# A new order of the work behind the last attention of a four-layer network, with products that nobody reads

## The chip, the cores and the metric

The kernel runs on one core of one Trainium2 chip, as one launch. The metric is the device time of an execution in microseconds (us). The engines are called by short names: PE is TensorE (PEld its weight loads), DVE is VectorE, ACT is ScalarE, POOL is GpSimd, and SP is SyncE, which here only orders transfers. Each engine works through its own queue in order. An instruction at the head of a queue that waits for a semaphore holds up all behind it.

## The reference

The input `x` has the shape [4, 56, 56, 128] in float32: 4 images of 3136 tokens with 128 channels. Four layers follow one another; all products are in single precision in the reference.

```python
x = neighbourhood_attention_and_mlp(x)                    # layer 0
x = x + gated_recurrence(group_norm(x))                   # layer 1, 16 steps
t = tokens(x)
t = t + softmax_attention(norm(t))                        # layer 2
t = t + top2_of_8_experts(norm(t))                        # layer 2, "mixture"
t = t + distance_attention(norm(t))                       # layer 3
t = t + experts_choose_tokens(norm(t))                    # layer 3
```

The last two matter here.

- Distance attention: Q, K and V are products of the tokens. The scores are exp(-|q - k|^2), and a softmax over them weighs V. Where all distances are large, every score is near zero, the softmax is uniform, and the result is the mean of V over the image.
- Expert choice: a router gives each token 64 logits; softmax runs over the tokens of an image. Each of 64 experts picks the 8 tokens of an image with the largest share, and the weighted sum of these ("pooled") goes through its own two layers, 129 to 512 with gelu, then 513 to 128. The result times each token's share is added to that token's row of the output.

## The kernel before

A tile is 112 tokens (`P`); an image has 28 tiles in 7 groups (`NG`) of 4 (`GT`). All images stay in SBUF as `env.x[b]`. The work on images 0 to 2 of layers 2 and 3 runs in the background of the attention of later images. What the change moves is the work on the last image, behind the last attention, where nothing is left to run beside it. It stands in a `tc.manual_schedule` block: the order in the program is the order in the queues of PE, DVE, ACT and POOL.

The order of that block before the change:

1. The last group of `Mixture`. `all_experts(g, j)` multiplies tile j by all 8 expert matrices (`y_ps`, L1563, two PSUM tiles of four experts), gates them (ACT at L1570 for j = 1 and 3, DVE at L1576 for j = 0 and 2) and adds them up (L1582, L1585). Then the normalization for layer 3 (`xn`, L1677 on POOL and L1682 on ACT), transposes (`xT_ps`, L207) and the queries and keys.
2. `FarAttention.mean()` (L1869 to L1876): the mean of V. `add(g)` (L1881) adds it to x, groups 0 to 2 on DVE, groups 3 to 6 on POOL.
3. `ExpertChoice.steps`, with a step function for each of these names: `statistics(g)` (sums for the norm), `root(groups)` (inverse standard deviation; groups 0 to 2 are "early", 3 to 6 "late"; DVE, in twelve instructions, then the offset at L2296), `store` (rows of x to DRAM, for the gather), `tokens(g)` (xn), `turned(g)` (transposes, copied to `zT` at L2311), `logits(g)` (L2316), `choose` (the 8 best of each expert, and four indirect DMAs on POOL at L2344 that fetch their rows), `marked` (which tokens are chosen), `weighed`, `gather` (copies the fetched rows and weighs them, L2372 to L2378), `pooled` (L2383 to L2388).
4. `experts()`: 16 steps of 4 experts for all four images. `first(q)` is the first layer (`h_ps`, L2431, copied at L2438), `turned(q)` the transposes, bias and gelu (L2444 to L2459), `second(q)` the second layer (`o_ps`, L2465, copied to `found` at L2471) and four small transfers of `found` into `out`, one for each image (L2478). The weights come in 32 lots of 1 MB, two for each step, into 9 buffers; `more` orders the next on SP (L2252) when a buffer is free. `second` runs two steps behind `first`.
5. `far.decide()` (L1921 to L1934) looks whether all distances were large; if not, another branch repeats the attention in full.
6. `scatter()`: for each pair of images, a product that picks the last results (L2501), the bias (L2504), then for each group products of the shares with the results (`y_ps`, L2518). Half of the results of most groups is copied by ACT (L2527) and added to x by POOL (L2528); the others are added by DVE (L2530). Each [112, 4, 128] block goes out from SP (L2531).

Beside these there are bound tiles: a matrix of |q - k|^2 must be bounded to decide step 5. `bounds(g, c, parts)` multiplies 32 rows of q by k (`d_ps`, L1850), and then either DVE takes the maximum (`tensor_reduce`, L1856) or ACT a sum of relus (L1862). For the last image there are 175 such tiles in 91 lists called `halves`. `beside(by, n)` puts the next n lists at a place of the order, where `by` is "scalar" (all on ACT) or "both" (alternating DVE and ACT). The lists that are left are spread over the steps of `experts()`, every third as "scalar".

The normalization of layers 2 and 3 for one group of tokens is in `span_norms`: DVE works out variance and mean, POOL takes the power -0.5 (L1662), and DVE forms the offset from it:

```python
nc.gpsimd.tensor_tensor(rs, var, env.exponent[:P, :n], ALU.pow)
out["off"] = off = small.tile([P, n], F32, tag=f"g_off{n}_{places}", name="g_off")
nc.vector.scalar_tensor_tensor(off, mean2, -0.5, rs, ALU.mult, ALU.mult)
```

It is called for a single group at 17 places, 15 of them beside attention.

Of the kernel before, what the change touches and what calls it, by code (L numbers as in the profile page):

```python
# [924 lines left out]

def moments(env, pool, tag, st):
# [510 lines left out]
class Mixture:  # L1437
# [41 lines left out]
    def parts(self, b, span, places):  # L1479
# [73 lines left out]
        def all_experts(g, j):  # L1553
            gate = held["gate"][:, span.index(g) * GT + j, :]
            gated = sp.tile([P, NE, C], F32, tag="gated", name="gated")
            by_scalar = shared and j % 2
            for i in range(2):
                if by_scalar:
                    pool, tag = (flow.ps_scores, "s") if j == 1 else (flow.ps_sums, "o")
                    y_ps = pool.tile([P, 4, C], F32, tag=tag, name="y_ps")  # L1560
                else:
                    y_ps = flow.one([P, 4, C], "y_ps")
# [4 lines left out]
                if by_scalar:  # L1567
# [79 lines left out]
def span_norms(env, small, b, span, places, shift=0.0):  # L1647
# [4 lines left out]
    def take():  # L1652
# [5 lines left out]
        if n > GT:  # L1658
            inverse_root(env, small, var, rs)
        else:  # L1660
            nc.vector.tensor_scalar(var, var, 1e-5, None, ALU.add)  # L1661
            nc.gpsimd.tensor_tensor(rs, var, env.exponent[:P, :n], ALU.pow)  # L1662
        out["off"] = off = small.tile([P, n], F32, tag=f"g_off{n}_{places}", name="g_off")
        nc.vector.scalar_tensor_tensor(off, mean2, -0.5, rs, ALU.mult, ALU.mult)  # L1664
# [542 lines left out]
class ExpertChoice:  # L2207
# [46 lines left out]
    def pieces(self, b, places="d"):  # L2254
# [5 lines left out]
        for g in range(NG):  # L2260
# [5 lines left out]
            costing(5.0, steps["choose"]), costing(5.0, steps["marked"]),  # L2266
            *[costing(0.7, lambda g=g: steps["weighed"](g)) for g in range(NG)],
# [3 lines left out]
    def steps(self, b, places, norms_of):  # L2271
# [20 lines left out]
        def root(groups):  # L2292
            of = slice(groups[0] * GT, (groups[-1] + 1) * GT)
            mean2, var = moments(env, sp, f"c{len(groups)}", st[:, of, :])
            inverse_root(env, sp, var, rs[:, of])
            nc.vector.scalar_tensor_tensor(off[:, of], mean2, -0.5, rs[:, of], ALU.mult, ALU.mult)  # L2296
# [53 lines left out]
        def marked():  # L2350
# [8 lines left out]
            nc.vector.reciprocal(inverse, total)  # L2359
# [20 lines left out]
        def pooled():  # L2380
# [13 lines left out]
            logits=logits, choose=choose, marked=marked, weighed=weighed, gather=gather,  # L2394
            pooled=pooled,
        )

    def experts(self, ctx, pool, units, others=()):
# [19 lines left out]
        h, g, used = {}, {}, set()  # L2418
# [42 lines left out]
        def second(q):  # L2461
# [14 lines left out]
            for b in range(B):  # L2476
                at = b % 2 * EC + ET * q
                nc.sync.dma_start(self.outs[b // 2][at : at + ET], by_image[b])  # L2478

        others = Paced(list(others))  # L2480
        slots = 3 * (NQ + 2)
        for q in range(NQ + 2):
            others.step((3 * q + 1) / slots)
# [3 lines left out]
            others.step((3 * q + 2) / slots)  # L2487
            if 0 < q <= NQ:
                turned(q - 1)
            others.step((3 * q + 3) / slots)  # L2490
            if q > 1:
                second(q - 2)
                more(2 * (q - 2) + 1)

    def scatter(self):

        env, nc, flow = self.env, self.env.nc, self.flow
        for pair in range(2):
# [4 lines left out]
            bias = self.late.tile([2 * EC, C], F32, tag="c_bias", name="c_bias")  # L2503
            nc.vector.tensor_scalar(bias, self.bias2, self.inverse[pair], None, ALU.mult)  # L2504
            nc.vector.scalar_tensor_tensor(
                out, out, self.inverse[pair], bias, ALU.mult, ALU.add
            )
            for g in range(NG):
                tiles = slice(g * GT, (g + 1) * GT)
# [12 lines left out]
                for half in range(2):  # L2522
                    b = 2 * pair + half
                    x = env.x[b][:, tiles, :]
                    if half and g not in (3, NG - 1):
# [355 lines left out]
def run_all(pieces):  # L2881
    for piece in pieces:
        piece()


def layers_of_safe_scores(env: Env, f, soft):
    with ExitStack() as ctx:
# [84 lines left out]
        choice, far = held["choice"], held["far"]  # L2972
# [8 lines left out]
        ]  # L2981

# [5 lines left out]
        with tc.manual_schedule(  # L2988
# [6 lines left out]
            beside("scalar", 5)  # L2995
            run_all(tail[:6])
            run_all(tail[6:10])
# [4 lines left out]
            choice.weights(more, range(UNITS))  # L3002
            mean()
# [3 lines left out]
            def each(name, groups):  # L3007
                run_all([lambda g=g: of[name](g) for g in groups])
# [3 lines left out]
            for g in early:  # L3012
                add[g]()
                of["statistics"](g)
                beside("scalar", 1)
            of["root"](early)
            of["store"](early)
            each("statistics", late)
            beside("scalar", 1)
            of["tokens"](0), of["tokens"](1), of["turned"](0), of["logits"](0)  # L3020
            of["root"](late)
            of["store"](late)
            of["turned"](1), of["tokens"](2), of["logits"](1), of["turned"](2), of["logits"](2)
# [96 lines left out]
```

## Time and profile before

| what | us |
|---|---|
| median of 3 runs | 2468.28 (2467.14 to 2473.53) |
| the profiled execution, its own time | 2469.86 |
| its span in the trace | 2467.9 |
| PE busy | 2337.2 (95%) |
| DVE busy | 1806.8 (73%) |
| ACT busy | 1560.5 (63%) |
| POOL busy | 289.6 (12%) |
| work behind the last attention, 2247.05 to the end | 220.85 |

The span is what the trace covers; the execution's own time is 2 us longer. The profile is one execution. The page's second part shows the busy share in 40 equal slices of the span, as digits in tenths; PEclk is the clock that TensorE was granted. Other views give busy time of each engine in chosen stretches, groups of instructions, waits, the chain of work that ended last, and a timeline.

### The profile page before, as it was taken

The numbers are of one execution on the slowest core, as the hardware profiler recorded it, in microseconds if no ns is written. First come the engines' busy times: TensorE is split into PE (matmuls) and PEld (weight loads), VectorE is DVE, ScalarE is ACT, GpSimd is POOL, SyncE is SP. The second block draws the span as 40 slices with busy tenths as digits, with TensorE's granted clock in tenths as the row PEclk, the third lists the DMA queues.
The fourth block names the chain that finished last, engine by engine and source line by source line (L and its number), as shares of the span: only waits on it lengthen the run. The fifth ranks groups of instructions, "written<-read, shape, count | busy, mean of one in ns | idle before, by whom it ended". The sixth has DMA issues, their size and how long they took to land.

```text
span 2467.9 us, 38789 instructions
## 1 busy us (share of the span) xinstructions
PE 2337.2 (95%) x14357; PEld 1256.4 (51%) x14357; DVE 1806.8 (73%) x4798; ACT 1560.5 (63%) x3382; POOL 289.6 (12%) x578
## 2 busy tenths in 40 slices
PE   5999999999999999999999999999999998997585
PEld 3777777775555555555554444445444433343134
DVE  5566899983898859699678777854788676775554
ACT  3899889875675646666432556575545566764583
POOL 4323354320000000000000000100000001012202
PEclk9999999999999999999999999999999998998587
DMA  6000000000000000000000010000000010101585
GB/s 143 14 10 2 2 2 2 2 2 9 1 1 1 1 1 0 1 1 1 12 1 0 1 27 1 5 1 1 1 1 1 1 27 5 27 5 53 151 304 177
DMA packets 65642, 61.42 MB, mean 25 GB/s; under 512 B 17048, under 2 KB 60915, under 8 KB 61348
## 3 DMA queue, kind: packets, MB, share of 16 engines
q1 hardware_dynamic: 64932, 57.80, 8.2%
q8 instruction: 115, 1.88, 0.3%
q0 software_dynamic: 512, 1.06, 0.2%
q14 instruction: 83, 0.68, 0.1%
HBM read 45.83 MB, written 12.90 MB: 24 GB/s over the span
## 4 chain that ended last, share of the span: by engine, by line
PE 63%; DVE 6%; ACT 3%; DMA 2%; POOL 1%; issue 1%; SPq 0%; DVEq 0%; ACTq 0%; POOLq 0%
PE s_ps L2055 20%; PE o_ps L2138 20%; PE y_ps L1563 7%; PE d_ps L1850 3%; PE xT_ps L207 2%; PE g_ps L1196 2%; DMA lot<-in_L_ffn_lots 1%; PE l_ps L2316 1%; ACT d_ps L1862 1%; PE y_ps L2079 1%; PE q_ps L1814 1%; PE z_ps L2031 1%; PE l_ps L1523 1%; ACT xn L1682 1%; DVE found L1856 1%
## 5 line engine op out<-in xcount | busy, mean ns | idle before, releaser
L2062 ACT ACTIVATE e<-s_ps 128x448 f32<-128x448 f32 x688 | 366.9, 542 | 501.4 <-PE s_ps L2055 495.9
L2055 PE MATMUL s_ps<-zT,xnT 128*128 128x448 f32 (+1 forms) x1400 | 648.7, 553 | 0.0
L2138 PE MATMUL o_ps<-e,keep 128*128 128x448 f32 (+1 forms) x1376 | 647.3, 553 | 0.0
L2138 PEld LDWEIGHTS o_ps<-e,keep 128*128 128x128 f32 (+1 forms) x1376 | 241.8, 190 | 218.4 <-issue 217.9
L2055 PEld LDWEIGHTS s_ps<-zT,xnT 128*128 128x128 f32 (+1 forms) x1400 | 241.4, 189 | 214.0 <-issue 194.3
L1862 ACT ACTIVATE d_ps<-d_ps,half 128x448 f32<-128x448 f32 (+1 forms) x394 | 238.5, 607 | 80.9 <-PE d_ps L1850 79.8
L1856 DVE TENSOR_REDUCE found<-d_ps 128x1 f32<-128x448 f32 x306 | 185.7, 618 | 86.8 <-PE d_ps L1850 84.8
L1563 PE MATMUL y_ps<-experts,xnT 128*112 128x512 f32 x448 | 216.3, 607 | 0.0
L1576 DVE TENSOR_TENSOR gated<-y_ps,gate 112x512 f32<-112x512 f32 x220 | 148.4, 685 | 34.1 <-PE y_ps L1563 31.8
L1850 PE MATMUL d_ps<-q_near,k_near 32*128 32x448 bf16 (+1 forms) x700 | 138.1, 379 | 20.9 <-ACT d_ps L1862 13.7
L1582 DVE TENSOR_TENSOR gated<-gated 112x512 f32<-112x512 f32 x330 | 150.7, 464 | 3.3
L207 PE MATMUL xT_ps<-ident,xn 112*128 112x112 f32 x672 | 117.3, 282 | 35.2 <-ACT xn L1682 27.1
L207 PEld LDWEIGHTS xT_ps<-ident,xn 112*128 112x128 f32 x672 | 80.3, 147 | 114.2 <-ACT xn L1682 60.0
L1662 POOL TENSOR_TENSOR g_rs<-var,exponent 112x4 f32<-112x4 f32 x17 | 17.9, 1054 | 993.3 <-DVE var L1661 882.3
L1563 PEld LDWEIGHTS y_ps<-experts,xnT 128*112 128x112 f32 x448 | 77.2, 180 | 98.6 <-issue 62.2
L1850 PEld LDWEIGHTS <-k_near 32*128 32x128 bf16 (+1 forms) x700 | 32.2, 92 | 182.1 <-issue 168.9
L675 DVE TENSOR_TENSOR e<-e,band 112x1792 f32<-112x1792 f32 (+3 forms) x56 | 100.0, 1789 | 15.3 <-ACT e L668 15.3
L1682 ACT ACTIVATE xn<-x,g_off,g_rs 112x128 f32<-112x128 f32 x220 | 93.2, 486 | 28.0 <-DVE g_off L1664 13.1
L780 PE MATMUL f_ps<-w_fc,h 128*112 128x128 f32 x896 | 104.8, 274 | 1.9 <-ACT h L771 1.6
L780 PEld LDWEIGHTS f_ps<-w_fc,h 128*112 128x112 f32 x896 | 99.8, 177 | 5.2 <-ACT h L771 4.8
L766 PE MATMUL h_ps<-zT,w_fc 128*128 128x448 f32 x224 | 88.9, 540 | 0.6 <-ACT zT L760 0.6
L668 ACT ACTIVATE e<-s_ps 112x1792 f32<-112x1792 f32 (+3 forms) x56 | 82.7, 1477 | 5.6 <-PE s_ps L659 2.5
(427 smaller groups left out, 3936.9 us busy)
## 6 DMA issues: line engine op xcount, KB each, us to landing
lot<-in_L_ffn_lots SPq DMA_DIRECT2D x32, 1024.0 KB
out_x<-x SPq DMA_DIRECT2D x28, 224.0 KB
x<-in_x SPq DMA_DIRECT2D x3, 1568.0 KB
rows<-x SPq DMA_DIRECT2D x3, 1568.0 KB
x<-in_x SPq DMA_DIRECT2D x7, 224.0 KB
parts<-in_waves SPq DMA_DIRECT2D x8, 173.0 KB
out<-found SPq DMA_DIRECT2D x60, 2.0 KB
rows<-x SPq DMA_DIRECT2D x1, 896.0 KB
```

The source lines that it names most:

```text
L207: self.nc.tensor.transpose(ps[:, j * P : (j + 1) * P], xn[:, j, :], self.ident[:P, :P])
L780: nc.tensor.matmul(f_ps[:, j, :], h[:, k, j * P : (j + 1) * P], w_fc2[:, k, :], start=(k == 0), stop=(k == 3),)
L1563: nc.tensor.matmul(y_ps, held["xnT"][g][:, j * P : (j + 1) * P], self.experts[:, 4 * i : 4 * i + 4, :], start=True, stop=True,)
L1576: nc.vector.tensor_tensor(gated[:, some, :], y_ps, gate[:, some].unsqueeze(2).to_broadcast([P, 4, C]), ALU.mult,)
L1582: by.tensor_tensor(gated[:, :n, :], gated[:, :n, :], gated[:, n : 2 * n, :], ALU.add)
L1682: env.nc.scalar.activation(xn[:, j, :], env.x[b][:, g * GT + j, :], AF.Identity, bias=norm["off"][:, i : i + 1], scale=norm["rs"][:, i : i ...
L1850: nc.tensor.matmul(d, held["k"][part, 128 * c : 128 * c + n], held["q"][g][part, :], start=True, stop=True,)
L1856: nc.vector.tensor_reduce(self.found[:, self.most : self.most + 1], d, AX.X, ALU.max)
L1862: nc.scalar.activation(d, d, AF.Relu, bias=self.half[:n], accum_out=self.found[:n, self.sums : self.sums + 1],)
L2055: nc.tensor.matmul(s_ps[i * n : (i + 1) * n, :GW], self.xnT[:, at : at + n], zT, start=True, stop=True,)
L2062: nc.scalar.activation(e[:n], s_ps[:n, :GW], AF.Exp)
L2138: nc.tensor.matmul(sums[:, :GW], self.keep[:n, k, :], e[:n], start=(k == 0 and g - 1 not in pairs), stop=last,)
```

## The change

- A new function `power_on_gpsimd` makes the inverse root and the offset on POOL. It is used for every single group in `span_norms`, and for both roots of the last image.
- In the last mixture group, tiles j = 2 and 3 are gated by ACT for the first four experts and by DVE for the other four; j = 1 stays on ACT.
- The order behind the attention is written anew. Ahead of the mixture stand 2 lists of bound tiles and not 5. The statistics of the late groups come together, and then the late root; the seven groups of the router follow in an order with the xn of one or two groups ahead. `products` and `with_norms` of the last group (queries, keys and their norms) stand around `choose` and `marked`; the reciprocal of the softmax's sum is a step of its own, `inverted`. The six "both" lists ahead of `gather` give way to three "scalar" ones. `experts()` gets 79 lists, all "both": 72 tiles on DVE and 79 on ACT, where it was 48 and 91.
- 165 products `warm`, bf16, 128x128 by 256 columns, write PSUM tiles that nobody reads. They stand at thirteen places between the start of the block and `gather`.
- In `experts()`, `second` runs one step behind `first` (17 slots and not 18). The small `out` transfers move from SP's queue to POOL's. The biases for the scatter are made on POOL at the step q = 1.
- `far.decide` moves from ahead of `scatter` into its first pair, ahead of group 3. The path by ACT and POOL is taken for three groups of each pair and not five.

The diff, cut to its core:

```diff
+def power_on_gpsimd(env, mean2, var, rs, off, shift=0.0):
+    nc = env.nc
+    p, n = var.shape
+    nc.vector.tensor_scalar(var, var, 1e-5, None, ALU.add)
+    nc.vector.tensor_scalar(mean2, mean2, -0.5, None, ALU.mult)
+    nc.gpsimd.tensor_tensor(rs, var, env.exponent[:p, :n], ALU.pow)
+    nc.gpsimd.tensor_tensor(off, mean2, rs, ALU.mult)
+    if shift:
+        nc.gpsimd.tensor_scalar(off, off, 1.0, shift, ALU.mult, ALU.add)
...
-            by_scalar = shared and j % 2
+            by_scalar = shared and j == 1
...
-                if by_scalar:
+                if by_scalar or shared and j > 1 and i == 0:
                     for e in range(4):
...
-            inverse_root(env, sp, var, rs[:, of])
-            nc.vector.scalar_tensor_tensor(off[:, of], mean2, -0.5, rs[:, of], ALU.mult, ALU.mult)
+            if last:
+                power_on_gpsimd(env, mean2, var, rs[:, of], off[:, of])
...
             for b in range(B):
                 at = b % 2 * EC + ET * q
-                nc.sync.dma_start(self.outs[b // 2][at : at + ET], by_image[b])
+                nc.gpsimd.dma_start(self.outs[b // 2][at : at + ET], by_image[b])
...
-        for q in range(NQ + 2):
-            others.step((3 * q + 1) / slots)
+        for q in range(NQ + 1):
             if q < NQ:
                 first(q)
                 more(2 * q)
-            others.step((3 * q + 2) / slots)
-            if 0 < q <= NQ:
-                turned(q - 1)
-            others.step((3 * q + 3) / slots)
-            if q > 1:
-                second(q - 2)
-                more(2 * (q - 2) + 1)
+            others.step((q + 0.3) / NQ)
+            if q == 1:
+                self.biases()
+            if q > 0:
+                second(q - 1)
+                more(2 * (q - 1) + 1)
+            if q < NQ:
+                turned(q)
+            others.step((q + 1) / NQ)
+
+    def biases(self):
+        nc = self.env.nc
+        for pair in range(2):
+            bias = self.bias2 if pair else self.late.tile([2 * EC, C], F32, tag="c_bias", name="c_bias", bufs=1)
+            nc.gpsimd.tensor_scalar(bias, self.bias2, self.inverse[pair], 0.0, ALU.mult, ALU.add)
+            self.bias.append(bias)
...
             for g in range(NG):
+                if (pair, g) == (0, 3):
+                    between()
...
-                    if half and g not in (3, NG - 1):
+                    if half and g in (0, 2, 4):
...
+        def warm(n):
+            ps = flow.ps_sums.tile([128, 512], F32, tag="o", name="warm_ps")
+            for _ in range(n):
+                nc.tensor.matmul(
+                    ps[:, :256], far.norm[:, 0, :], far.norm.rearrange("p i c -> p (i c)"),
+                    start=True, stop=True,
+                )
...
-            beside("scalar", 5)
-            run_all(tail[:6])
-            run_all(tail[6:10])
+            beside("scalar", 2)
+            warm(20)
+            run_all(tail[:3])
+            warm(3)
+            run_all(tail[3:10])
+            warm(50)
             run_all(tail[10:])
...
+            warm(4)
             mean()
...
                 beside("scalar", 1)
+                warm(6)
             of["root"](early)
             of["store"](early)
-            each("statistics", late)
-            beside("scalar", 1)
-            of["tokens"](0), of["tokens"](1), of["turned"](0), of["logits"](0)
+            each("s3 s4 s5 s6 n0")
             of["root"](late)
             of["store"](late)
...
+            for _ in range(3):
+                beside("scalar", 1)
+                warm(6)
+            each("n1 t0 t1 l0 n2 t2 l1 l2 n3 t3 n4 t4 l3 n5 t5 l4 n6 t6 l5 l6")
+            of["choose"]()
+            products()
             beside("scalar", 1)
...
-            of["choose"]()
-            beside("scalar", 2)
-            products()
+            warm(16)
             of["marked"]()
             with_norms()
-            beside("both", 6)
+            of["inverted"]()
+            beside("scalar", 1)
+            warm(16)
+            beside("scalar", 2)
+            warm(20)
             of["gather"]()
             of["pooled"]()
-            others = [
-                lambda i=i, half=half: half("scalar" if i % 3 == 2 else "both")
-                for i, half in enumerate(halves)
-            ]
+            others = list(halves)
...
-            far.decide()
-            choice.scatter()
+            choice.scatter(far.decide)
```

In the string of the router's order, n is `tokens`, t `turned`, l `logits` and s `statistics`, each with its group.

## Prediction

> **What bounds the kernel now.** I read the page first, then busy time by stage behind the last attention, the clock in short windows, SP's waits, and POOL's timeline.
>
> ```profile
> span 2467.9 us, 38789 instructions
> PEclk9999999999999999999999999999999998998587
> ```
>
> Until 2247 us TensorE is busy (9 in nearly every slice) and the clock is full. The last 221 us are another program; the clock row falls to 5 there. Columns of the windows: length; busy PE, PEld, DVE, ACT, POOL; granted clock; DMA share; GB/s.
>
> ```profile
> 2247.05:2273.22 26.17, 15.96 (x39) 6.31 (x38) 13.84 (x50) 12.14 (x40) 7.73 (x11) 0.71 0.00 0
> 2273.22:2289.42 16.20, 4.80 (x14) 1.57 (x14) 11.04 (x46) 7.09 (x22) 8.74 (x9) 0.50 0.93 376
> 2289.42:2316.60 27.18, 19.99 (x47) 6.71 (x48) 9.88 (x38) 14.36 (x33) 5.65 (x13) 0.50 0.78 184
> 2316.60:2336.09 19.49, 9.09 (x29) 2.35 (x29) 14.96 (x27) 11.18 (x27) 5.09 (x11) 0.50 0.05 14
> 2336.09:2431.27 95.18, 79.39 (x843) 33.13 (x841) 47.95 (x87) 75.63 (x214) 0.00 (x0) 0.84 0.70 256
> 2431.27:2467.90 36.63, 17.10 (x230) 15.90 (x230) 15.07 (x31) 6.41 (x12) 12.59 (x10) 0.75 0.68 179
> ```
>
> In order: last mixture group; mean and norms; seven router products; choice and gather; 16 steps of four experts; scatter. No engine is full in the first four: they are chains of short dependent instructions, three of them wholly at half clock. The experts are uneven: ACT 75.63 of 95.18 us, DVE 47.95. Which wait ends last there:
>
> ```profile
> SPq L2478 <- DMA lot<-in_L_ffn_lots: 20.1, 14, 2.3
> SPq L2478 <- DVE found L2471: 9.8, 7, 2.2
> 2375.37 9.71 DMA lot<-in_L_ffn_lots
> 2386.79 7.59 DMA lot<-in_L_ffn_lots
> ```
>
> The small `out` transfers (L2478) stand in SP's queue ahead of the weight orders and wait there for `found` (in total 20.1 + 9.8 us); the chain of waits then runs through the weight lots, 7.6 to 9.7 us at a time. So SP's order, not bandwidth, delays weights.
>
> **The change part by part.** Sums are made against the profiled span, 2467.9 us. That run took 2469.86, the median of the runs is 2468.28, so I take median = span + 0.4.
>
> *The 165 products without a reader.* They are bf16, 128x128 by 256 columns. The norm product (448 columns) starts every 0.19 us at full clock: 0.107 us each, twice that at half, so 18 to 35 us of TensorE. The chains leave it idle: in the second stage it is busy 4.80 of 16.20 us. What they buy is the clock:
>
> ```profile
> 2255.85:2261.50 5.65, 5.65 (x13) 3.18 (x14) 3.14 (x17) 0.23 (x1) 0.00 (x0) 0.50 0.00 0
> 2270.00:2272.00 2.00, 0.00 (x0) 0.00 (x0) 0.00 (x0) 0.00 (x0) 1.86 (x2) 0.95 0.00 0
> 2314.00:2320.00 6.00, 5.03 (x17) 0.94 (x16) 3.96 (x4) 4.01 (x11) 0.00 (x0) 0.50 0.00 0
> 2354.00:2356.00 2.00, 1.29 (x12) 0.25 (x9) 1.37 (x3) 1.51 (x5) 0.00 (x0) 1.00 0.70 123
> ```
>
> 5.65 us of dense expert products raised it at 2261.5; it fell 5.4 us after the last of them (2271.9) and came back only at 2353.7. The Trainium skill ("TensorE: Matmul & The Clock Gate", Part 1, the HAM clock gate) says one busy window of about 3.4 us gives full clock and one idle window takes it away. By that rule 2314 to 2320 (5.03 of 6 us busy) should have raised it; the row says 0.50. Those were bound tiles (32 rows deep) and router products (64 columns of weights). So busy time alone isn't enough, and products over the whole array may be. The new ones are of that kind, but in packs of 6 (0.65 us at full clock) between gaps. By the rule the stages from 2273 to 2336 run at 1.00; by the row they may stay at 0.50. I take full clock as likelier and keep half clock as a rival.
>
> *Mixture, mean, norms.* (a) Ahead of xn 4 ACT relus stand instead of 10: ACT was the last to finish (2253.5); xn comes about 2.3 earlier. (b) Transposes and products at full clock (four transposes 1.02 to 0.55): -1.2. (c) The last two gating groups are split over ACT and DVE (11.3 to about 10.2 us): -1.1. (d) Second normalization and mean at full clock: -0.75, its offset on POOL +0.1. (e) The early root moves from DVE (12 instructions, 2.5 us) to a POOL power over 12 columns. The trace has 4 columns at 1.01 us and 28 at 4.81, hence 2.28 and, for 16 columns, 2.91 by interpolation. It queues behind POOL's four `x` adds (1.62 each): +0.3. (f) The late power (2.91, multiply 0.26) stands in POOL's queue ahead of the next group's xn: router products start only 1.3 earlier, so 3.6 of the 4.9 are given back.
>
> *Router products.* Seven of transpose, copy, logits; at half clock 3.4 us apiece (1.02 and 1.75 on TensorE), at full clock 2.4: 25.5 to 16.6 us, -8.9. At half clock I allow -3.2, for bound tiles no longer between them. *Choice to first expert.* The copy of the gathered rows waited on DVE until 2332.4 behind six reductions, though the last gather had landed near 2327.4 (2.5 us after its issue). The change puts three ACT relus and 52 products there instead: 19.5 to 14.2 us, -5.3. The sum is -15.5, with half clock about -10; unevenness takes some, so the first expert product comes at T0 = 2322 (-14).
>
> *Experts.* Bound tiles go from 48 DVE, 91 ACT to 72, 79. Four limits:
> - ACT: 12 tiles x 0.61 us less, 75.6 - 7.3 = 68 to 69 us; before, six compute-bound steps took 27.22 us with ACT 96% busy. T0 + 74.
> - DVE: 47.95 + 24 x 0.62 = 63, plus unevenness: T0 + 65.
> - Weights: 22 lots after the first at 2.5 to 2.74 us (measured at 2276 to 2290 and 2380 to 2400): T0 + 61 to 66.
> - POOL: 60 transfers of 4 x 512 B move to its queue from SP. The trace has no plain transfer issued there. The nearest row is the gather:
>
> ```profile
> 2322.44 0.94 POOL L2344 DMA_INDIRECT c_got<-rows,c_at  x1 [0.30 <-issue]
> 2323.69 0.95 POOL L2344 DMA_INDIRECT c_got<-rows,c_at  x1 [0.30 <-issue]
> ```
>
> 1.25 us from one to the next, and 0.94 of it is work with 128 rows; four descriptors may take 0.5. The skill ("DMA: Bandwidth & Descriptors", Anatomy of one DMA — SWDGE (gpsimd) path) states about 2.0 us fixed for each transfer issued from GpSimd, most of it the receipt of the write; the same page (SWDGE vs HWDGE vs iDMA) sends plain copies to SP or ACT: a rule against this edit. The gathers followed each other faster than they landed (2.5 us), so a receipt isn't waited for, and 2.0 is the upper end, for a queue that does wait. At 0.5 POOL hides behind ACT; at 1.25 it needs 75 us from the first `found` (T0 + 6.7), T0 + 82; at 2.0, T0 + 127. I take 1.25, the row: 95.2 to 82, -13. Two bias multiplies (0.4 each) on that queue count nothing.
>
> *Scatter.* Bias and `decide` leave its head (-1.6); DVE gets 22 of 28 adds instead of 18, POOL 6, four POOL adds of 1.28 less. It stays bound by writing `out_x`, 24 to 26 us; first write earlier and full clock another -2. -3.6: 33 us.
>
> *The fifteen norms beside attention* now put multiply (and shift) on POOL, 0.2 to 0.4 each, and take as much from DVE: nothing, as TensorE is the bound there at clock 0.99. With that cover gone, at most 15 x 0.25 = 3.7 us.
>
> Sum: -14 - 13 - 3.6 = about -31. Span 2322 + 82 + 33 = 2437; median about 2437.
>
> **The rivals.**
> - *ACT sets the pace.* POOL issues in under 1.1 us: T0 + 74, 2429. For it: only four descriptors. Against: the fixed part of an issue is all that two unlike rows would share.
> - *A loop of waits.* Each `second` stands one step behind `first` instead of two; h, gelu, turn, product now have less slack. At 5.5 us a step 16 steps take 88: 2443. For it: the long lot waits in the chain. Against: SP holds only weights now.
> - *The clock stays at half,* for the reason of the 2314 row. T0 2326, products at 0.21 us stand in the way of transposes, scatter 35: 2444 to 2450.
> - *No change.* The gains of the chains are given back to a late POOL queue: experts end near 2435 as before.
> - *Slower: POOL's issue price.* Experts can't end before T0 + 6.7 + 60p, since the scatter reads what these transfers bring. Break-even with before: (2435 - 2329) / 60, p = 1.77. At the page's 2.0, one transfer at a time, the end is 2329 + 120 + 33 = 2482. Against it: the row of 1.25 with 32 times the rows.
> - *The change doesn't do what it says:* warm products held by their PSUM buffers. Only the pack of 50 waits for ACT to free one; it would then run late, in front of the next transposes, 5 us at most. This lies in the half-clock case.
>
> **How the numbers follow.** POOL-paced 0.38 (2437); ACT-paced 0.22 (2429); loop 0.14 (2443); half clock 0.14 (2450); no change 0.05; slower 0.07. A measurement of this kernel can tell 0.3%, 7.4 us, from no change. Faster 0.88, same 0.05, slower 0.07. Range: low end, ACT-paced with 70 us of experts and 31 of scatter, 2421; high end, half clock, the attention's cover gone and a little of the loop, 2456. Outside remain no change, slower, and a few per cent below 2421.
>
> **What would show it.** Right: clock at 0.9 or more from 2250 to T0; first expert product near 2322; `out` issues on POOL 1.0 to 1.3 us apart, and a chain through them; steps of 4.6 to 5.1 us; ACT and DVE within 10 us of each other in the experts; scatter 33. Wrong: clock 0.50 in the router products; transposes waiting behind products without a reader; `out` issues over 1.7 us apart; or lots still last in the chain. A first expert product not before 2330 would overturn the first half of the sum, experts over 90 us the second.

## The result, and the profile after

| | before | after |
|---|---|---|
| median of 20 runs, us | 2470.48 (2466.03 to 2478.71) | 2475.31 (2470.66 to 2482.21) |
| ratio to before | | 1.002 (95%: 1.0013 to 1.0028) |
| profiled execution, own time / span | 2469.86 / 2467.9 | 2480.35 / 2478.6 |

A gain of 31 us was forecast; the kernel became 0.2% slower, which lies within what was set as no change. The profiled execution of after is 5 us above its median, so its trace shows somewhat more loss than the runs do. The page of after:

```profile
span 2478.6 us, 39116 instructions
PEclk9999999999999999999999999999999998998777
```

The digits of PEclk for the last three of the 40 slices are 7, where before had 5, 8 and 7: the clock is not half any more, but it isn't full either. Where the time went is read from five places in PE's timeline: the end of attention, the first and the last logits product (`l_ps`), the first expert product (`h_ps`), the end of the last (`o_ps`). Stages in us, one profiled execution each:

| stage | before | after | forecast | measured |
|---|---|---|---|---|
| start to the end of attention | 2247.06 | 2246.11 | 0 | -1.0 |
| to the first logits product | 44.01 | 44.39 | -1.3 | +0.4 |
| seven router products | 24.29 | 21.58 | -8.9 | -2.7 |
| choice, to the first expert product | 20.73 | 19.19 | -5.3 | -1.5 |
| experts | 94.82 | 108.03 | -13 | +13.2 |
| scatter and end | 36.99 | 39.30 | -3.6 | +2.3 |

The sum is +10.7, the difference of the spans. The forecast is missed by 42 us in all, and 26 of these by the experts. Windows of after, with the columns of the prediction (length; busy PE, PEld, DVE, ACT, POOL; clock; DMA share; GB/s), for the router, the experts and the scatter:

```profile
2290.50:2312.08 21.58, 16.02 (x36) 5.16 (x35) 3.81 (x6) 10.64 (x22) 3.96 (x9) 0.58 0.70 103
2331.27:2439.30 108.03, 88.09 (x855) 38.44 (x855) 60.39 (x110) 69.37 (x191) 33.93 (x60) 0.78 0.64 226
2439.30:2478.60 39.30, 21.05 (x230) 19.57 (x230) 17.40 (x34) 3.52 (x6) 7.59 (x6) 0.72 0.64 167
```

In the experts ACT has 69.37 us (forecast 68 to 69), DVE 60.39 (63), POOL 33.93: the work is spread as the prediction had it, and no engine is full. So engines wait for one another. The chain of waits in after shows one turn of a ring that repeats step by step; each line is start, length, and what ran:

```profile
2382.57 0.70 PE hT_ps L2464 x4
...
2383.36 0.69 DVE c_g L2472
2384.06 1.07 DVE found L1867 x2
2385.13 0.04 issue
2385.17 0.34 PE d_ps L1861
2385.51 1.82 PE h_ps L2451 x8
2387.34 0.49 PE d_ps L1861 x3
2387.83 1.57 PE o_ps L2485 x32
2389.40 0.70 PE hT_ps L2464 x4
```

One turn takes 6.83 us, and nothing in it is a transfer or POOL. PE transposes h, DVE adds the bias (`c_g`) and only then takes two maxima (`found`); PE waits for these with the last of its bound tiles, and the next `h_ps` stands behind that tile in PE's queue. PE's own waits in this stage say the same (total, times, longest):

```profile
PE d_ps L1861 <- DVE found L1867: 18.9, 29, 1.9
PE hT_ps L2464 <- ACT c_h L2458: 0.7, 2, 0.5
```

Why the bound tiles wait is in the program's order. PE's queue, with H for `h_ps`, T for `hT_ps`, O for `o_ps` and the number of bound tiles between them, taken from the middle of the loop:

```
before  H 4 T 2 O 4 H 2 T 4 O 2 H 2 T 2 O 4 H
after   H 2 O T 8 H 2 O T 6 H 4 O T 8 H 2 O T 6 H
```

The pool of these tiles has four PSUM tiles (`f_ps4`, `bufs=4`). Four go through; the fifth to eighth wait until DVE or ACT has emptied one, and DVE has the bias add first. The order of before never puts more than four in a row, but for a few places at the ends. That the number of PSUM tiles is the limit is read from this order and the waits; a pool of another size was not tried.

### The profile page after: what moved, and what is told of

Read it like the earlier page. It is cut to its first block, busy times and chain, and to the rows that moved or that the text cites. A ratio compares the mean times of both kernels' runs of the same rounds, so it can differ in the third digit from the quotient of the medians.

```text
span 2478.6 us, 39116 instructions
## 1 busy us (share of the span) xinstructions
PE 2361.3 (95%) x14522; PEld 1280.7 (52%) x14522; DVE 1813.3 (73%) x4790; ACT 1547.8 (62%) x3342; POOL 331.1 (13%) x663
## 4 chain that ended last, share of the span: by engine, by line
PE 63%; DVE 8%; ACT 2%; issue 2%; POOL 1%; DMA 0%; DVEq 0%; ACTq 0%; POOLq 0%
PE s_ps L2066 19%; PE o_ps L2149 19%; PE y_ps L1575 7%; PE d_ps L1861 3%; PE xT_ps L207 2%; PE g_ps L1208 2%; DVE found L1867 1%; PE l_ps L2333 1%; PE o_ps L2485 1%; PE q_ps L1825 1%; PE y_ps L2090 1%; PE z_ps L2042 1%; PE h_ps L2451 1%; PE l_ps L1535 1%; DVE gated L1588 1%
## 5 line engine op out<-in xcount | busy, mean ns | idle before, releaser
L1873 ACT ACTIVATE d_ps<-d_ps,half 128x448 f32<-128x448 f32 (+1 forms) x376 | 226.8, 603 | 85.1 <-PE d_ps L1861 82.9
L1867 DVE TENSOR_REDUCE found<-d_ps 128x1 f32<-128x448 f32 x324 | 195.0, 619 | 82.6 <-PE d_ps L1861 80.5
L1861 PE MATMUL d_ps<-q_near,k_near 32*128 32x448 bf16 (+1 forms) x700 | 130.0, 373 | 35.8 <-DVE found L1867 20.3
L932 POOL TENSOR_TENSOR g_rs<-var,exponent 112x4 f32<-112x4 f32 x17 | 21.3, 1250 | 992.6 <-DVE var L930 909.2
```

What stands on the lines that cost most here:

```text
L1861: nc.tensor.matmul(d, held["k"][part, 128 * c : 128 * c + n], held["q"][g][part, :], start=True, stop=True,)
L1867: nc.vector.tensor_reduce(self.found[:, self.most : self.most + 1], d, AX.X, ALU.max)
L1873: nc.scalar.activation(d, d, AF.Relu, bias=self.half[:n], accum_out=self.found[:n, self.sums : self.sums + 1],)
```

## The experiments

Medians are in us, of 4 to 13 executions of each new kernel; the ratio is to the kernel before on the same chip, with its 95% interval. Times of stages are those of one profiled execution.

How far a stage's time can be trusted shows where several kernels share its code. Five of them (after, `after_old_loop`, `after_lag1_three`, `after_lag2_two`, `ol_pool_split`) are the same up to the experts: the first logits product came 43.65 to 45.49 us behind the end of attention, the first expert product 83.42 to 86.53 us. Differences of 2 us at the first place and 3 us at the second mean nothing by themselves.

### The experts

Theory A, formed from the above: the stop of 6 to 8 bound tiles in front of `h_ps` makes the ring. Rival B: the lag of one step does, or POOL's transfers.

`after_old_loop`: the loop of before in the kernel after.

```diff
-        for q in range(NQ + 1):
...
+        slots = 3 * (NQ + 2)
+        for q in range(NQ + 2):
+            others.step((3 * q + 1) / slots)
...              # first(q), more(2q), biases at q = 1
+            others.step((3 * q + 2) / slots)
...              # turned(q - 1)
+            others.step((3 * q + 3) / slots)
...              # second(q - 2), more
```

> The kernel after with the expert loop of before: three stops for bound tiles in each step (at most 4 tiles in a row between two expert products, but for three places), second two steps behind first; out transfers stay on POOL. Theory A (what costs the 108 us of experts is the stop of 6 to 8 bound tiles in front of the next h_ps, against 4 PSUM tiles, so that PE waits for DVE's reductions, which stand behind c_g): steps of about 4.5 to 5 us, experts 76 to 84 us, span 25 to 30 us under that of after. Rival B (POOL's out transfers, or the one-step lag alone): B with POOL leaves the experts at 100 us or more; B with the lag gives the same gain as A here.

`after_lag1_three`: the lag of one step stays, with three equal stops.

```diff
-            others.step((q + 0.3) / NQ)
+            others.step((q + 0.33) / NQ)
...
             if q > 0:
                 second(q - 1)
...
+            others.step((q + 0.67) / NQ)
             if q < NQ:
                 turned(q)
             others.step((q + 1) / NQ)
```

> The kernel after, second still one step behind first, but the bound tiles at three equal stops (after first, after second, after turned), so at most 4 in a row. Theory A (size of the stop): experts 76 to 86 us, nearly all the gain of the run with the old loop. Rival B (the lag of one step): the experts stay above 100 us.

`after_lag2_two`: lag of two steps, two uneven stops.

```diff
-        for q in range(NQ + 1):
+        for q in range(NQ + 2):
...
-            others.step((q + 0.3) / NQ)
+            others.step((q + 0.3) / (NQ + 1))
...              # second(q - 2), turned(q - 1)
-            others.step((q + 1) / NQ)
+            others.step((q + 1) / (NQ + 1))
```

> The kernel after, second two steps behind first as in the kernel before, but still two uneven stops, 5 to 8 bound tiles in a row ahead of h_ps. Theory A (size of the stop): experts stay above 100 us. Rival B (the lag): experts 76 to 86 us.

`before_pool_out`: the kernel before, out transfers on POOL.

```diff
-                nc.sync.dma_start(self.outs[b // 2][at : at + ET], by_image[b])
+                nc.gpsimd.dma_start(self.outs[b // 2][at : at + ET], by_image[b])
```

> The kernel before with one edit, the 60 out transfers issued by POOL and not by SP. The weight orders are then no longer behind transfers that wait for found. Expected: the lot waits of 2375 to 2395 and 2399 to 2419 go, experts 95 to about 78 to 82 us (ACT's pace of 4.5 to 5), time 12 to 16 us less. Rival (POOL's issue price of 1.25 us or more): experts not under 85 us. The trace of after has 0.57 us for one such issue, which speaks against the rival.

`before_new_loop`: the kernel before with the loop of after (without the biases).

> The kernel before with one edit, the expert loop of after (second one step behind first, two uneven stops: 4 to 6 bound tiles in a row ahead of h_ps); its out transfers on SP, its balance of DVE and ACT and everything else as before. Theory A (the stop of more tiles than PSUM holds): experts 100 to 110 us instead of 95, time 5 to 15 us more. Rival (the loss comes from the new parts together, such as DVE's larger share, and not from this loop): 95 us or less.

| kernel | tiles ahead of H | experts, us | PE busy | clock | median | ratio |
|---|---|---|---|---|---|---|
| before | 2 to 4 | 94.82 | 79.4 | 0.84 | | 1 |
| after | 6 to 8 | 108.03 | 88.1 | 0.78 | 2475.31 | 1.002 (1.0013 to 1.0028) |
| after_old_loop | 2 to 4 | 76.43 | 69.8 | 1.00 | 2449.42 | 0.9921 (0.9902 to 0.9941) |
| after_lag1_three | 2 to 4 | 79.31 | 72.0 | 1.00 | 2453.18 | 0.9927 (0.9905 to 0.9949) |
| after_lag2_two | 4 to 8 | 113.98 | 93.2 | 0.73 | 2476.49 | 1.0044 (1.0028 to 1.0061) |
| before_pool_out | 2 to 4 | 82.30 | 74.1 | 0.89 | 2457.25 | 0.9949 (0.9932 to 0.9966) |
| before_new_loop | 4 to 6 | 96.34 | 80.1 | 0.84 | 2471.98 | 1.0011 (1.0 to 1.0022) |

The lag makes no difference that shows, the size of the stop does: theory A holds, B falls. PE's waits for `found` in this stage agree: 2.2 us in `after_lag1_three`, 19.7 us in `after_lag2_two`. The profiled execution of `after_lag2_two` took 2491.35 us, 14.9 more than its median, so its 113.98 us is high; with all of that taken off, 99 us are left. PE's waits in `after_old_loop`, same stage:

```profile
PE d_ps L1861 <- ACT d_ps L1873: 3.6, 10, 0.5
PE d_ps L1861 <- DVE found L1867: 2.1, 5, 0.6
```

18.9 us of waiting for `found` became 2.1, and all idle time of PE in the stage 6.7 us, from 19.9. That is 13.3 us of the 31.6. The other 18.3 are the clock: the same products keep PE busy 88.1 us at 0.78 and 69.8 us at 1.00. That the waits are what lowers it was not tried by itself. A turn of after that ran at full clock (h_ps at 2407.68 to h_ps at 2412.92, 0.99) took 5.24 us, still more than the 4.78 of `after_old_loop` (76.43 / 16).

POOL's transfers hold nothing up. In after's groups, POOL's own (busy and mean ns, then idle before):

```profile
L2498 POOL DMA_DIRECT2D out<-found x60 | 33.9, 568 | 78.0 <-DVE found L2491 78.0
```

0.57 us each, 78 us idle. And moving them pays: with this one edit the experts of before go from 94.82 to 82.30 us.

`before_new_loop` missed its expectation of 100 to 110 us. In before the weights waited behind SP's out transfers, and PE waited 8.0 us in all for lots and 2.5 for `found`. With the new loop the chain has no lot in it: PE waits for no lot, 11.0 us for `found`, and a step takes 6.0 us. One wait took the place of the other at nearly the same price. So the new loop costs next to nothing in before; it costs where the wait for the weights is gone, as in after.

### From the mixture to the first expert

After's PE timeline at the two places where products without a reader meet a wait (start, length, operation; in brackets the idle time before and who ended it):

```profile
2279.02 0.83 PE L3015 MATMUL warm_ps<-norm 128*128 128x256 bf16 x6
2286.01 1.14 PE L1861 MATMUL d_ps<-q_near,k_near 32*128 32x448 bf16 x2 [6.17 <-ACT d_ps L1873]
...
2326.14 4.45 PE L3015 MATMUL warm_ps<-norm 128*128 128x256 bf16 x20
2330.38 0.53 PE L2407 MATMUL t_ps<-fold,c_got 128*128 128x64 f32 x2
```

At the first, six products stand behind a bound tile that waits for ACT. At the head of ACT's queue is the xn of group 0, which waits 5.78 us for the offset that POOL makes (L933). PE is idle for 6.17 us and the clock falls (1.00 until 2282, 0.50 from 2284). At the second, 20 products at half clock stand ahead of rows that DVE finished at 2327.3 (L2405 ran from 2326.97 for 0.34 us), and the next product starts 3 us late. In the router, after's chain is a ring again:

```profile
2302.95 0.54 ACT taken L2337
2303.48 0.02 issue
2303.50 0.50 ACT xn L1693
2304.00 0.04 issue
2304.05 1.02 PE xT_ps L207 x4
2305.07 1.70 PE l_ps L2333 x2
2306.76 0.02 issue
2306.79 0.54 ACT taken L2337
```

3.84 us a group: the copy of one group's logits stands on ACT ahead of the next group's xn, which PE needs for its transposes. In the new order xn is asked for only after the product before it.

`ol_no_warm`: after_old_loop without the 165 products.

> The kernel after with the expert loop of before (as in after_old_loop) and none of the 165 products without a reader. Theory C (they buy little because PE stands still at other waits, and cost where they stand in front of work that is ready): the first expert product comes 2 to 4 us earlier than in after_old_loop (83.9 us behind the attention's end), although mixture products run at half clock. Rival (they pay, by the clock): it comes 3 us later or more.

`ol_router`: after_old_loop with

```diff
-            each("n1 t0 t1 l0 n2 t2 l1 l2 n3 t3 n4 t4 l3 n5 t5 l4 n6 t6 l5 l6")
+            each("n1 t0 n2 t1 l0 n3 t2 l1 n4 t3 l2 n5 t4 l3 n6 t5 l4 t6 l5 l6")
...
-            warm(20)
             of["gather"]()
```

> The kernel after with the expert loop of before, and two edits in different stages: the router's groups with xn two groups ahead (n1 t0 n2 t1 l0 n3 t2 l1 and so on), so that ACT's copy of the logits no longer stands ahead of the xn that the next transposes need; and without the 20 products directly ahead of gather. Theory D (the router is a ring of four waits through ACT, 3.84 us a group, which leaves PE idle for 1.14 us in each and the clock at half): logits 21.4 to about 15 to 19 us. Theory E (the 20 products stand in front of the pooled rows, which are ready 3 us before): choice 18.5 to about 15.5 us. Rival to D (the half clock alone sets 3.4 us a group): logits stay above 20 us.

`r_beside_late`: ol_router with

```diff
-            for _ in range(3):
-                beside("scalar", 1)
-                warm(6)
+            warm(18)
...
             products()
-            beside("scalar", 1)
+            beside("scalar", 4)
```

> The kernel ol_router with the three lists of bound tiles that stand between the late root and the router (six relus, 3.7 us of ACT between the xn of group 0 and that of group 1) moved behind choose. Theory H (they stand on ACT ahead of the xn that the router waits for): first logits product 44.2 to about 40.5 to 42 us behind the attention's end, and the first expert product 2 to 3.5 us earlier. Rival (POOL's late power of 2.9 us, queued ahead of group 1's xn, sets it): no change over 1 us.

`r_no_warm`: ol_router without any of the products.

> The kernel ol_router without any of the products that nobody reads. With the old router order their loss moved the first expert product by under half a microsecond. Theory I (once the router is no ring, TensorE is busy enough to raise its clock by itself): router 12 to 14 us, first expert product within 2 us of ol_router's 73.2 us. Rival (here the products pay, since the clock is granted because of them): router 16 us or more, or the first expert product 3 us later.

`n_all` is r_no_warm with the three lists moved as in r_beside_late, and `decide` in the second pair (see the scatter); `n_root_dve` is n_all with

```diff
-            if last:
+            if False:
                 power_on_gpsimd(env, mean2, var, rs[:, of], off[:, of])
             else:
...
```

> n_decide_p1 with the three lists of bound tiles ahead of the router moved behind choose, now without warm products. Theory H again, in a kernel whose PE has nothing else in its queue there: the first logits product 44.9 to 41 to 42.5 us behind the attention's end; time 2436 to 2440. Rival (POOL's late power, ahead of group 1's xn on its queue, is next in line): no change over 1 us against n_decide_p1.

> n_all with both roots of the last image on DVE again (twelve instructions), not a POOL power. If POOL's 2.28 and 2.90 us are what the router waits for (the prediction gave back 3.6 us of the front for it), the first logits product comes 1 to 3 us earlier. Rival (DVE, which also makes the late statistics, is no quicker there): same or later.

Measured from the end of attention:

| kernel | first logits | router | choice | first expert | experts | median | ratio |
|---|---|---|---|---|---|---|---|
| after_old_loop | 43.95 | 21.42 | 18.49 | 83.86 | 76.43 | 2449.42 | 0.9921 |
| ol_no_warm | 45.02 | 21.68 | 16.81 | 83.51 | 82.61 | 2453.62 | 0.9944 (0.9926 to 0.9962) |
| ol_router | 44.20 | 12.20 | 16.81 | 73.21 | 83.62 | 2445.90 | 0.9914 (0.9895 to 0.9933) |
| r_beside_late | 43.69 | 12.56 | 16.38 | 72.63 | 81.17 | 2442.60 | 0.9893 (0.9870 to 0.9916) |
| r_no_warm | 44.94 | 11.95 | 16.80 | 73.69 | 80.91 | 2441.44 | 0.9890 (0.9867 to 0.9913) |
| n_all | 44.76 | 11.94 | 16.75 | 73.45 | 81.55 | 2444.05 | 0.9897 (0.9875 to 0.9919) |
| n_root_dve | 40.85 | 13.99 | 16.74 | 71.58 | 82.41 | 2441.34 | 0.9885 (0.9863 to 0.9906) |

The router was the ring: 21.4 to 12.2 us by order alone, and 11.95 us with no product that keeps the clock. The window of ol_router's seven groups:

```profile
2289.13:2301.33 12.20, 11.45 (x36) 3.86 (x35) 3.62 (x6) 10.24 (x22) 3.91 (x9) 0.86 1.20 198
```

PE is busy 11.45 of 12.20 us and the clock is mostly full (0.86). r_no_warm, with no pack at all, is as quick. In after PE was busy 16.02 of 21.58 us and the clock was 0.58. The 20 products cost 1.7 us of the choice (18.5 to 16.8). All 165 together change nothing that shows: the first logits product comes at 43.95 with them and 45.02 without, the first expert product at 83.86 and 83.51, both inside the spread given above. `ol_no_warm` didn't reach its expected 2 to 4 us, and the rival's 3 us of loss isn't there either. The medians disagree on the sign: in the old router order 0.9944 without and 0.9921 with the products, in the new one 0.9890 without and 0.9914 with most of them, and the intervals overlap. (The experts' 82.61 against 76.43 us is taken up below.)

What the router's start waits for: moving six relus off ACT alone brought 0.5 us (`r_beside_late`) or 0.2 (`n_all`), which is nothing against the spread. With the roots on DVE too it came 3.9 us earlier (`n_root_dve`), and as early in `best_b` below (41.01). The chain of n_all shows why theory H fell:

```profile
2288.44 0.04 POOL c_rs L932
2288.48 2.90 issue
...
2291.41 0.22 POOL c_off L933
2291.63 0.44 POOL xn L1688
```

The 2.90 us after L932's start are the POOL power over 16 columns; the xn of the next group stands behind it in POOL's queue. On DVE the late root is itself later, so the router becomes 13.99 us and the first expert gains 1.9 of the 3.9.

### The scatter

`ol_pool_split`: after_old_loop with

```diff
-                    if half and g in (0, 2, 4):
+                    if half and g not in (3, NG - 1):
```

> The kernel after with the expert loop of before, and the scatter's path by ACT and POOL for five groups of a pair again, not three (DVE adds 18 of 28). Theory F (DVE's 22 adds make the blocks too slowly, so that the output transfers have gaps): from the last expert product to the end 40 to about 36 us. Rival (the gaps come from the half clock and from decide in the middle): stays at 38 to 40.

`r_decide_end`: ol_router with `between()` behind both loops; `r_both` has r_beside_late's edit as well; `n_decide_p1` is r_no_warm with

```diff
-                if (pair, g) == (0, 3):
+                if (pair, g) == (1, 1):
                     between()
```

> The kernel ol_router (old expert loop, router two groups ahead, no products ahead of gather) with decide behind the last group of the scatter and not ahead of group 3 of the first pair. Theory G (decide stops DVE and PE for 2 us in the middle, blocks come late, the output transfers get gaps and the clock does not rise): from the last expert product to the end 37.8 to 34.5 to 36 us. Rival (the half clock or the split sets it): 37 us or more.

> Both edits of r_decide_end and r_beside_late on ol_router. If theories G and H hold, 4 to 6 us less than ol_router: about 2440 us, 1.1% under the kernel before. If neither holds, 2446.

> The kernel r_no_warm (old expert loop, router two groups ahead, no products without a reader) with decide at group 1 of the second pair. In r_decide_end the output transfers had no gaps and ended 29.6 us behind the last expert product (after: about 35), but the end came 12 us behind them, since reading the flag and the branch then start late. Theory K (decide in the middle of pair 0 makes the gaps; in pair 1 the transfers have a backlog, and the branch is still hidden): from the last expert product to the end 37.5 to 34 to 35.5 us. Rival (the half clock at the start of the scatter makes the gaps wherever decide stands): 37 us or more.

From the last expert product to the end, us: before 36.99, after 39.30, after_old_loop 39.99, ol_router 37.84, r_no_warm 37.49; `ol_pool_split` 40.82; `r_decide_end` 41.48, `r_both` 41.83; `n_decide_p1` 38.79. Medians: ol_pool_split 2452.96 (0.9942, 0.9919 to 0.9965), r_decide_end 2448.54 (0.9921, 0.9897 to 0.9946), r_both 2449.38 (0.9923, 0.9903 to 0.9942), n_decide_p1 2444.34 (0.9898, 0.9876 to 0.9919).

None of the theories F, G and K held as put, but `r_decide_end` separates two things. Busy share of the DMA engines in 40 slices, of before from 2428 to 2470 us, of after from 2436 to 2480 us, and of r_decide_end from 2400 to 2445 us:

```profile
DMA  0000000001779999999999999999899995000000
```

```profile
DMA  0000000066999549889994699999986999100000
```

```profile
DMA  0000002599999999999999999999511000000000
```

With `decide` in the first pair (after) the output transfers have gaps (5, 4, 4, 6). With it at the head (before) or at the end (r_decide_end) they have none. The last slice at 9 ends 31.7 us behind the last expert product in before, 34.1 in after and 29.8 in r_decide_end, where a thin rest follows (5, 1, 1, to 2434.9). But there the flag `again` is written only at 2428.2 (L1945), where the chain of waits ends, and the program ends at 2443.2, 8 us behind that rest; after ends 4 us behind its last slice. The likely reading is that what follows the flag, reading it and the branch, takes long and is hidden only if `decide` comes early. In the second pair (`n_decide_p1`) the transfers had a gap again and the end lay no better.

Why each place costs what it does was not settled, and one rival stands: the clock. Ten of the kernels have the scatter of after to the letter, and took from 36.84 us (after_lag1_three, clock 0.80) to 39.99 (after_old_loop, clock 0.72), 38.25 in the mean. The three with the scatter of before took 36.99, 37.03 and 37.44 us, 37.15 in the mean.

### A better version

Without the pack ahead of `gather` the experts begin at half clock, so it might pay after all. `best_a` is after_old_loop with ol_router's order only, all products kept; `best_b` has of the products only the 16 and 20 behind `inverted`, roots on DVE, and the three lists moved.

> The kernel after with the expert loop of before and the router two groups ahead; all 165 products stay, also the 20 directly ahead of gather. Theory L (the products ahead of gather cost 1.7 to 3 us of waiting, but put the clock at full for the start of the experts, where without them the first 20 us run at half): choice 18 to 19 us instead of 16.8, experts 75 to 78 us instead of 81 to 84; 2 to 5 us under ol_router. Rival (the clock at the start of the experts comes from the slower router, or is chance): experts 80 us or more.

> best_a with only the two packs behind inverted (16 and 20 products) of the 165, both roots of the last image on DVE, and the three lists of bound tiles ahead of the router moved behind choose. If L holds and 36 products are enough: first expert product 72 to 74 us behind the attention's end, experts 75 to 78, time 2434 to 2440 us. Rival: the clock needs the earlier packs too, experts 80 us or more, 2441 us.

best_a: choice 18.59, experts 81.60 us, 2446.86 (0.9885, 0.9856 to 0.9914). best_b: choice 18.53, experts 81.28 us, 2440.34 (0.9862, 0.9836 to 0.9887). The first 10 us of best_b's experts, and of r_no_warm's:

```profile
2319.13:2329.13 10.00, 8.11 (x49) 2.15 (x48) 7.52 (x14) 9.63 (x26) 0.00 (x0) 0.93 0.68 222
```

```profile
2318.20:2328.20 10.00, 8.28 (x38) 1.88 (x38) 6.51 (x12) 7.82 (x20) 0.00 (x0) 0.58 0.59 183
```

The clock does start higher (0.93 against 0.58), but ACT is then busy 9.63 of the 10 us, in the next 10 us of best_b the clock is back at 0.73, and the experts are no shorter: theory L falls. That after_old_loop's experts took 76.43 us stays one execution's number; the same experts took 79.84 in `ol_pool_split`. best_b has the lowest ratio. It and six others with the loop of before and the new router order lie within 0.9862 to 0.9898, with intervals that overlap, so which of the seven is best isn't shown.

## Why the prediction was wrong, point by point

- **What bounds the kernel.** Right for the experts: SP's order delayed the weights (before_pool_out, 0.9949). The router did run at half clock, and PE stood idle in it for 5.8 of 24.29 us. A small misreading: the clock before 2247 us was not full throughout; from 2060 to 2120 us before had 0.86.
- **Experts, the failing step.** The sum listed four limits, ACT, DVE, weights, POOL, and took the largest, 82 us with POOL. None of the four held the stage up: POOL's 1.25 us an issue measured 0.57, ACT and DVE were within 3 us of their forecast, and with the same four `after_old_loop` took 76.43 us. The fifth limit was left out: the order within PE's queue against the four PSUM tiles of the bound tiles. It cost 19.9 us of idle PE and, with the clock at 0.78, 108.03 us. The rival "a loop of waits" named the right kind of cause, but put it on the lag and at 5.5 us a step; it was the uneven stops, and 6.75 us (108.03 / 16).
- **Router.** "At full clock 2.4 us a group" took the clock as given by the products. It stayed at 0.58, because PE waited for ACT's queue in every group. The order alone brought 21.4 to 12.2 us: PE's idle time fell from 5.6 to 0.8 us (after_old_loop, ol_router), and its busy time from 15.9 to 11.5 as the clock rose to 0.86. The products brought nothing that could be measured. The rule from the Trainium skill ("TensorE: Matmul & The Clock Gate", Part 1, the HAM clock gate) and the row from 2314 us were weighed as if one must be false. They don't contradict each other, because the rule asks for sustained work. In these traces the granted clock changes on a grid of 3.41 us. On that grid PE was busy 2.42 us in one of before's stretches (2312.75 to 2316.17) and 2.76 us in the next, so neither was full. An average hides this: in ol_router PE was busy for 93% from 2328.14 to 2338.14, at a clock of 0.55. Of the stretches there only the third was full, and the clock rose right behind it:

```profile
2326.80:2330.21 3.41, 2.88 (x13) 0.34 (x13) 1.62 (x3) 2.72 (x8) 0.00 (x0) 0.50 0.52 211
2330.21:2333.63 3.42, 2.71 (x18) 1.09 (x18) 1.72 (x3) 1.94 (x5) 0.00 (x0) 0.50 0.67 206
2333.63:2337.04 3.41, 3.41 (x44) 1.51 (x38) 2.09 (x5) 2.35 (x6) 1.00 (x2) 0.50 0.50 144
2337.04:2340.45 3.41, 3.41 (x56) 1.73 (x52) 2.62 (x7) 2.94 (x9) 1.36 (x3) 1.00 0.95 374
```

  In all 19 traces, from 2240 us on, 144 stretches at half clock had PE busy for 98% or more, and 127 of them were followed by full clock; of 254 with PE busy for less than 85%, 2 were. So "busy time alone isn't enough" isn't borne out: it depends on where the busy time lies. What decided the 17 exceptions, and the stretches between, stays open. In after's router PE was busy 16.02 of 21.58 us, with no pack among the groups to fill the gaps, so nothing was there to raise the clock.
- **Choice.** -5.3 became -1.5; without the pack of 20 it was about -4 (16.4 to 16.8 us). The copy of the gathered rows did come free of DVE's reductions, but the pack of 20 products was put on the path instead. The prediction had priced packs in the way only in its half-clock rival, 5 us at most.
- **POOL's roots.** Sizes right (2.28 and 2.90 us, as interpolated), and the 3.6 us that they give back were of the right size: `n_root_dve` found 3.9, in another kernel. The start of the router, -1.3 in the forecast and +0.4 here, is inside the spread.
- **Scatter.** -3.6 became +2.3 in this pair of executions, and +1.1 between the means above. The head gained the 1.6 us (first output transfer 4.9 us behind the last expert product, 6.5 before), but the full clock that was to bring 2 us did not come (0.72). The gaps stand where `decide` was put, and the prediction named no one who waits for it there; how much of the loss is these gaps and how much the clock isn't shown.
- **Norms beside attention.** Not resolved: in these profiles the end of attention lies at 2242.7 to 2253.8 us, in all kernels alike.

## What to carry to other kernels

When work is rearranged between engines, count along the in-order queue of the engine in the middle: how many tiles of one pool stand in a row, how many buffers the pool has, and what the engine that frees them has to do first. Where no engine of a stage is full, look for a ring of waits; its period can be added up from one turn of the chain. Here idle time of TensorE was better removed by asking for its inputs one group earlier than filled with products that nobody reads: filler in an in-order queue waited with everything else, and was then in the way.

## What the runs showed of the hardware

- A plain transfer of 2 KB issued by POOL takes POOL 0.57 us, about six tenths of what a gather of 128 rows took (0.94 to 1.08). POOL does not wait for its landing (4.5 us in the median, while four are issued in 2.38).
- The granted clock rose behind 127 of 144 stretches of 3.41 us in which PE was busy for 98% or more, and behind 2 of 254 in which it was busy for less than 85% (19 traces, from 2240 us on). An average over ten microseconds hides this: ol_router had 93% and 0.55.
- With the flag for a branch written late, the program ended 15 us behind DVE's write of it, 8 of these behind the last output transfers (r_decide_end).
